# Adding the row term of a graph-attention layer with bf16 parts and a 0/1 map instead of small f32 matmuls

## The chip, the cores and the metric

The kernel runs on one NeuronCore of one Trainium2 chip. The metric is the device time of one execution in microseconds (us); the figure for a kernel is the median over its runs. The profile shows one such execution: the span from its first to its last instruction, and what each engine did in it. The engines are TensorE (PE, with its weight loads shown as PEld), VectorE (DVE), ScalarE (ACT), GpSimd (POOL) and SyncE (SP, which issues the DMAs here).

## The reference, cut to what matters

Sixteen graphs (`b`) of 1024 nodes with 64 features pass through two attention layers, each followed by a residual add and a layer norm. Each row of the adjacency matrix has a few non-zero entries. Layer 0 is an eight-head dot-product attention. Layer 1, which the change touches, is this:

```python
hp = einsum('bni,oi->bno', h, lin_w) + lin_b
W1, W2 = W_w[:, :64], W_w[:, 64:]
u = hp @ W1.T                       # one term for each row i
v = hp @ W2.T                       # one term for each column j
s = u[:, :, None, :] + v[:, None, :, :]
s = where(s > 0, s, 0.2 * s)
e = einsum('bijf,f->bij', s, a)
e = where(adj > 0, e, -9e15)
h_prime = softmax(e, axis=2) @ hp
out = elu(h_prime)                  # then x + out, layer norm
```

## The kernel before

**Rows, groups and slots.** The 1024 rows of a graph are cut into 8 tiles of 128 rows; a tile holds 64 rows from each half of the graph, so partitions 0 to 63 belong to one half (`n` = 0) and 64 to 127 to the other. Eight neighbouring rows form a group (`GR` = 8; `NQ` = 8 groups in each half of a tile). For each group the kernel builds on the device a list of the columns that any of its rows needs; with the group's own eight rows this gives `SLOTS` = 120 slots to a group. A mask (bf16, 0 where the row has the edge of that slot, `NEG` = -2^100 elsewhere) says which of the group's slots belong to which row. If a list overflows, a second, full routine runs instead; in the runs shown it is only tested for.

**The two layers.** `prepare` builds the lists and `finish` the masks. `gather` (L504) fetches the features of all slots by a matmul of the features with 0/1 columns `f`, which DVE makes in `indicate` (L480, bf16, 2176 elements each). So that bf16 matmuls keep f32 accuracy, the features are split by `thirds` into three bf16 parts, `x3`, on POOL: copy to bf16 (L453), subtract (L456), copy, subtract, copy, one operation at a time. The gathered features land in `xg` (64 features on the partitions of each half, 8 groups by 120 slots).

In layer 1, `sums` computes `u` once for a graph (f32, PSUM to SBUF by DVE, L733). For each tile `own_rows` makes two things: `ub` on POOL (L738, f32, 128x512: the tile's `u`, copied to each of the 8 groups and multiplied by `in_q`, which is 1 where the row belongs to that group and 0 elsewhere) and `rw` on ACT (L743, f32, 128x120: the mask turned to 1 where the row has the slot and 0 elsewhere). `project` then computes, for each group, v of its slots plus u of the row that owns the slot: 4 f32 matmuls of 480 columns (L750) start the sums in the two PSUM tiles `pz`, and 16 f32 matmuls of 120 columns (L756), one for each group, add `ub` of that group times `rw`. A single f32 matmul leaves two records in the trace, so the page counts 32 for each call at L756. All of them work on a quarter of the PE array (64 rows by 64 columns) in the order of `CORNERS`, so that four in a row lie in different quarters.

After `project` comes the leaky ReLU: ACT `r` (L761), then DVE `r` (L762), twice each. Then `weigh` (L776) contracts with `a`, adds the mask, and DVE takes the row maximum; `exps` (ACT), `turn_weights` (PE transpose L790, DVE copy `eT` L792), `attend` (L801) follow one or two steps later. `weigh` and `turn_weights` share one PSUM buffer (tag "e", one buffer), so that L776 has to wait until `eT` of the tile before has been copied.

**The order.** All five engines run queues written out by hand in one loop over steps `g`; `t` = `g` mod 8 is the position of a step. Layer 0 works on tile `g`, layer 1 on tile `u` = `g` - 12. A step issues, among others: `project(u-1)`, `place(g,1)`, `gather(u,0)`, `turn_weights`, `turn`, `place(g,2)`, `weigh(u-1)`, `gather(u,1)`, `place(g,3)`, `indicate`, `own`, `own_rows(u)`, `attend`, `place(g,4)`, and in the next step `place(g,0)`, `score`, `divide`. `place` is where the pieces of list building for the next graph are put in (in particular L325, L363 to L371, L345, L378, L380 on DVE and L328 on POOL), and where one operation of the list `lists.side` is taken: this is how the `thirds` operations are spread, one to a place:

```python
            while self.side:
                if next(self.side[0], 0) is None:
                    break
                self.side.pop(0)
```

Each engine takes its instructions strictly in the order in which they were issued. `sums` of a graph is called at the end of the step with `t` = 3, the first `own_rows` of that graph stands in the step with `t` = 4, and its first `project` in that with `t` = 5.

Of the kernel before, what the change touches and what calls it, by code (L numbers as in the profile page):

```python
# [9 lines left out]
F32 = mybir.dt.float32  # L10
I32 = mybir.dt.int32
AF = mybir.ActivationFunctionType
ALU = mybir.AluOpType
# [3 lines left out]
NEG = -(2.0**100)  # L17
# [12 lines left out]
BF16 = mybir.dt.bfloat16  # L30
# [3 lines left out]
def kernel(  # L34
# [4 lines left out]
    nc = tc.nc  # L39
    B, N, D = x.shape  # L40
    H = edge_bias.shape[1]
    HD = H * D
    P = 128
    NT = N // P
# [16 lines left out]
    ones = cst.tile([P, P], F32, name="ones")  # L61
# [3 lines left out]
    def sub(n):  # L65
        return slice(n * D, n * D + D)
# [41 lines left out]
    for h in range(H):  # L108
        c, r = h // 2, sub(h % 2)
# [73 lines left out]
    NQ = D // GR  # L183
# [33 lines left out]
    in_q = fst.tile([P, NQ], F32, name="in_q")  # L217
# [32 lines left out]
    SLOTS = 2 * CAP2 + GR  # L250
# [9 lines left out]
    dbl = fast.enter_context(tc.tile_pool(name="g_dbl", bufs=2))  # L260
# [21 lines left out]
    inputs, started, edges, masks, late = {}, {}, {}, {}, {}  # L282
# [160 lines left out]
        nc.vector.tensor_tensor(bad, bad, fl, ALU.max)  # L443
        masks[b] = mask

    def thirds(src, tag, nm):

        t3 = dbl.tile([P, 3, NT, D], BF16, tag=tag, bufs=3, name=f"{tag}_{nm}")
        less = per.tile([P, NT, D], F32, tag="less", name=f"less_{tag}_{nm}")

        def parts(rest):
            for k in range(3):
                nc.gpsimd.tensor_copy(t3[:, k, :, :], rest)  # L453
                yield
                if k < 2:
                    nc.gpsimd.tensor_tensor(less, rest, t3[:, k, :, :], ALU.subtract)  # L456
                    rest = less
                    yield

        return t3, parts(src)  # L460

    class Tiles:
# [63 lines left out]
        def begin(self, x_):  # L526

            b = self.b
            px = ps_g.tile([P, 512], F32, tag="g", name=f"px{self.layer}_{b}")
            columns_T(px, x_)  # L530
            self.xT = dbl.tile([P, 512], F32, tag=f"xT{self.layer}", bufs=2 - self.layer, name=f"xT{self.layer}_{b}")
            nc.scalar.copy(self.xT, px)
            self.t3, parts = thirds(x_, "x3", f"{self.layer}_{b}")
            self.f, self.xg, self.xn = {}, {}, {}
            lists.side.insert(0, parts)

    def banks(tag, name):

        return [ps_s.tile([P, 4, SLOTS], F32, tag=tag, name=f"{name}_{n}") for n in range(2)]
# [177 lines left out]
    class Layer1(Tiles):  # L717
# [9 lines left out]
        def sums(self):  # L727
            pu = ps_g.tile([P, NT, D], F32, tag="g", name=f"pu_{self.b}")
            for t in range(NT):
                for n in range(2):  # L730
                    nc.tensor.matmul(pu[sub(n), t, :], self.xT[:, ts(t, D)], w1h[:, n, :], start=True, stop=True)
            self.u = dbl.tile([P, NT, D], F32, tag="u", bufs=1, name=f"u_{self.b}")
            nc.vector.tensor_tensor(self.u, pu, rows_b[:, 0:1, :].to_broadcast([P, NT, D]), ALU.add)  # L733

        def own_rows(self, t):
            nm = f"{self.b}_{t}"
            ub = dbl.tile([P, NQ, D], F32, tag="ub", name=f"ub_{nm}")
            nc.gpsimd.tensor_tensor(  # L738
                ub, self.u[:, t, :].unsqueeze(1).to_broadcast([P, NQ, D]), in_q.unsqueeze(2).to_broadcast([P, NQ, D]),
                ALU.mult,  # L740
            )
            rw = dbl.tile([P, SLOTS], F32, tag="rw", name=f"rw_{nm}")
            nc.scalar.activation(rw, masks[self.b][:, t, :], AF.Identity, bias=ones[:, 0:1], scale=-1.0 / NEG)  # L743
            self.rows_[t] = ub, rw

        def project(self, t):
            xg, (ub, rw) = self.xg[t], self.rows_.pop(t)
            pz = banks("s", f"pz_{self.b}_{t}")
            for n, c_ in CORNERS:
                nc.tensor.matmul(  # L750
                    pz[n][sub(c_), :, :], w2d[sub(n), :],
                    xg[sub(n), :, :].rearrange("p (g c) k -> p c g k", c=2)[:, c_, :, :], start=True, stop=False,
                )
            for p in range(4):
                for n, c_ in CORNERS:
                    nc.tensor.matmul(  # L756
                        pz[n][sub(c_), p, :], ub[sub(n), 2 * p + c_, :], rw[sub(n), :], start=False, stop=(p == 3)
                    )
            self.r[t] = [dbl.tile([P, 4, SLOTS], F32, tag="r", bufs=3, name=f"r_{self.b}_{t}_{n}") for n in range(2)]
            for n, r in enumerate(self.r[t]):  # L760
                nc.scalar.activation(r, pz[n], AF.Relu)  # L761
                nc.vector.scalar_tensor_tensor(r, pz[n], SLOPE / (1.0 - SLOPE), r, ALU.mult, ALU.add)  # L762
# [117 lines left out]
    lists = Lists()  # L880
    with tc.manual_schedule(engines={getattr(mybir.EngineType, e) for e in order}):
# [12 lines left out]
        for g in range(NT * B + LAG + 7):  # L894
            u = g - LAG
            b, t = divmod(g, NT)
# [472 lines left out]
```

## Time and profile before

| | |
|---|---|
| median of 3 runs | 2506.59 us (2506.02 to 2509.31) |
| profiled execution | 2508.34 us, span 2506.5 us, mean granted PE clock 0.987 |
| PE busy | 2296.7 us (92% of the span) |
| PEld busy | 1951.9 us (78%) |
| DVE busy | 1930.4 us (77%) |
| ACT busy | 1450.3 us (58%) |
| POOL busy | 1010.8 us (40%) |
| L756 | 4096 PE records, mean 263 ns |
| L738 on POOL | 128 instructions, mean 1209 ns |

A record's duration includes its way through the array, and four of them overlap, so the 263 ns at L756 are not what each adds: the starts of records and of the group that follows tell that. "Idle before" is the time for which an engine stood still before an instruction, with the one that let it go. Until about 290 us only the lists of the first graph and layer 0 run; from about 2360 us on only layer 1 is left.

### The profile page before, as it was taken

How to read it: one execution, taken by the hardware profiler on the slowest of the kernel's cores; microseconds unless marked ns; L12 is line 12 of the kernel's file. 1: busy time of each engine (PE TensorE's matmuls, PEld its weight loads, DVE VectorE, ACT ScalarE, POOL GpSimd, SP SyncE). 2: the span in 40 equal slices, each digit the busy share in tenths (PEclk: the TensorE clock that was granted, in tenths of full speed). 3: DMA queues.
4: the chain of work that ended last, by engine and by line, in shares of the span. 5: the costliest groups of instructions: out<-in, count | busy, mean ns of one | idle time of the engine just before them, and what ended most of it. 6: DMA issues, size and time to landing. Idle time of an engine off the chain costs nothing.

```text
span 2506.5 us, 111153 instructions
## 1 busy us (share of the span) xinstructions
PE 2296.7 (92%) x48706; PEld 1951.9 (78%) x48706; DVE 1930.4 (77%) x5237; ACT 1450.3 (58%) x4401; POOL 1010.8 (40%) x1490
## 2 busy tenths in 40 slices
PE   5377999999999999999999999999999999999996
PEld 3266778888887888878888887878888887888864
DVE  6586868888887888888788878878787887866543
ACT  0054565666565665656566665656566665666743
POOL 1033433535344353534445353444534444443431
PEclk9988999999999999999999999999999999999998
DMA  3313242333224233323324232332423233231211
GB/s 102 109 43 117 81 143 77 104 116 109 91 81 138 77 117 103 121 77 100 120 77 140 81 119 77 113 107 78 142 86 113 83 111 103 66 96 61 69 38 29
DMA packets 192705, 239.03 MB, mean 95 GB/s; under 512 B 91732, under 2 KB 157332, under 8 KB 192212
## 3 DMA queue, kind: packets, MB, share of 16 engines
q1 hardware_dynamic: 192212, 231.85, 30.3%
q8 instruction: 384, 6.29, 1.0%
q14 instruction: 109, 0.89, 0.1%
HBM read 226.58 MB, written 5.21 MB: 92 GB/s over the span
## 4 chain that ended last, share of the span: by engine, by line
PE 66%; DVE 25%; DMA 3%; ACT 2%; issue 2%; POOL 1%; SPq 0%; POOLq 0%; ACTq 0%; DVEq 0%
PE pg L504 21%; PE s L616 5%; PE pt L523 5%; PE z L668 5%; DVE r L762 4%; PE pz L750 4%; PE pp L658 4%; PE pa L801 4%; PE pq L599 4%; PE pz L756 4%; PE po L684 3%; PE e L776 3%; DVE f L480 3%; DMA ad<-in_adj_dram 2%; PE pat L334 2%
## 5 line engine op out<-in xcount | busy, mean ns | idle before, releaser
L504 PE MATMUL pg<-f,x 128*64 128x272 bf16 (+2 forms) x13312 | 806.1, 273 | 40.4 <-DVE f L480 34.6
L504 PEld LDWEIGHTS <-x 128*64 128x64 bf16 x13312 | 662.8, 109 | 119.2 <-issue 73.8
L650 POOL TENSOR_TENSOR ls<-ls,den 128x480 f32<-128x480 f32 x256 | 298.5, 1166 | 579.8 <-DVE den L649 577.0
L510 ACT COPY xg<-pg 128x448 f32<-128x448 f32 x512 | 271.8, 531 | 392.4 <-PE pg L504 392.2
L480 DVE TENSOR_SCALAR f<-cb,jrow 128x2176 bf16<-128x2176 bf16 x512 | 409.0, 843 | 1.2 <-DMA cb<-col_d 1.0
L642 ACT ACTIVATE ls<-ls,mx 128x120 f32<-128x120 f32 x1024 | 391.2, 386 | 0.0
L524 ACT COPY xn<-pt 120x512 f32<-120x512 f32 x512 | 277.9, 598 | 22.7 <-PE pt L523 21.0
L523 PE MATMUL pt<-ident,xg 128*120 128x128 f32 x2048 | 269.6, 274 | 0.4
L761 ACT ACTIVATE r<-pz 128x480 f32<-128x480 f32 x256 | 132.2, 568 | 220.3 <-PE pz L756 220.3
L523 PEld LDWEIGHTS pt<-ident,xg 128*120 128x120 f32 x2048 | 229.4, 138 | 7.3 <-ACT xg L510 2.8
L489 POOL COPY xg<-xT 128x64 f32<-128x64 f32 x256 | 98.8, 396 | 307.1 <-PE pt L523 307.1
L762 DVE SCALAR_TENSOR_TENSOR r<-pz,r 128x480 f32<-128x480 f32 x256 | 155.9, 651 | 74.9 <-ACT r L761 74.6
L624 DVE TENSOR_TENSOR sc<-s,rowc 128x480 f32<-128x480 f32 x256 | 155.5, 649 | 71.2 <-PE s L616 69.3
L642 ACT ACTIVATION_READ_ACCUMULATOR ls<-ls,mx 128x1 f32 x1024 | 194.5, 190 | 0.0
L558 POOL TENSOR_TENSOR rs<-mv,eps 128x2 f32<-128x2 f32 x128 | 32.3, 253 | 379.0 <-DVE den L649 299.4
L632 DVE SCALAR_TENSOR_TENSOR ls<-sc 128x480 f32<-128x480 f32 x256 | 175.7, 686 | 0.0
L633 DVE TENSOR_REDUCE mx<-ls 128x4 f32<-128x480 f32 x256 | 167.2, 653 | 8.8
L756 PEld LDWEIGHTS pz<-rw,ub 64*64 64x64 f32 x4096 | 118.8, 133 | 63.2 <-issue 62.2
L600 DVE TENSOR_TENSOR qp<-pq,qb 128x512 f32<-128x512 f32 x128 | 88.2, 689 | 102.2 <-PE pq L599 101.0
L668 PE MATMUL z<-w,xn 120*64 120x64 f32 x4096 | 160.2, 229 | 4.8 <-ACT w L660 4.0
L658 PE MATMUL pp<-ident,ls 128*120 128x128 f32 x1024 | 143.0, 281 | 22.9 <-POOL ls L650 16.0
L668 PEld LDWEIGHTS z<-w,xn 120*64 120x64 f32 x4096 | 139.0, 141 | 28.6 <-ACT w L660 26.0
(212 smaller groups left out, 4092.7 us busy)
## 6 DMA issues: line engine op xcount, KB each, us to landing
cb<-col_d SPq DMA_DIRECT2D x271, 544.0 KB
ad<-in_adj_dram SPq DMA_DIRECT2D x256, 256.0 KB
xs<-in_x_dram SPq DMA_DIRECT2D x32, 128.0 KB
rows_s<-slot_d SPq DMA_DIRECT2D x256, 14.0 KB
out_dram<-o SPq DMA_DIRECT2D x32, 128.0 KB
col_d<-col SPq DMA_DIRECT2D x128, 4.2 KB
dg<-in_adj_dram SPq DMA_DIRECT2D x32, 2.0 KB
slot_d<-slot SPq DMA_DIRECT2D x16, 28.0 KB
```

Of the source, the lines that this page charges most:

```text
L480: nc.vector.tensor_scalar(fj.rearrange("p s n q k -> p (s n q k)"), cb.rearrange("p s n q k -> p (s n q k)"), jrow[:, j : j + 1], None, AL ...
L504: nc.tensor.matmul(pg[sub(n), :, FIRST * a_ + lo : FIRST * a_ + to], self.t3[:, k, 4 * hs + 2 * a_ + j, :], f[j][:, 2 * hs + a_, n, :, lo:to],
L510: nc.scalar.copy(dst, pg)
L523: nc.tensor.transpose(pt[:, q, :], xg[:, 4 * m + q, :], ident)
L524: nc.scalar.copy(self.xn[t][:, ts(m, 4), :], pt)
L632: nc.vector.scalar_tensor_tensor(ls, scs[n], SLOPE, scs[n], ALU.mult, ALU.max)
L642: nc.scalar.activation(ls[:, q, :], ls[:, q, :], AF.Exp, bias=neg[:, q : q + 1], accum_out=den[:, q : q + 1])
L650: nc.gpsimd.tensor_tensor(ls, ls, den.unsqueeze(2).to_broadcast([P, 4, SLOTS]), ALU.mult)
L658: nc.tensor.transpose(pt[:, p, :], ls[:, p, :], ident)
L668: nc.tensor.matmul(zz[sub(n), q, :], xn[:, q, sub(n)], w_[n][:, q // 2, sub(q % 2)], start=True, stop=True)
L756: nc.tensor.matmul(pz[n][sub(c_), p, :], ub[sub(n), 2 * p + c_, :], rw[sub(n), :], start=False, stop=(p == 3))
L762: nc.vector.scalar_tensor_tensor(r, pz[n], SLOPE / (1.0 - SLOPE), r, ALU.mult, ALU.add)
```

## The change

`u` is split once for a graph into three bf16 parts `u3` by `thirds` (two buffers), whose five POOL operations (three of L453, two of L456, 128x512 each) go to the front of `lists.side` after `sums` at the end of `t` = 3. `own_rows` makes `rw` in bf16 on ACT first, and from it, on POOL, a map `rq` (bf16, 128x960: `rw` repeated for the 8 groups and multiplied by `in_q`). `project` adds `u` with 3 rounds of 4 bf16 matmuls of 480 columns, in place of 16 f32 matmuls of 120 columns; each takes one part of the tile's `u` as weights and the map of four groups as the moving operand. `ub` goes. On POOL `rq` stands where `ub` stood; it now follows an ACT instruction of the same step, which `ub` did not.

```diff
-    def thirds(src, tag, nm):
+    def thirds(src, tag, nm, bufs=3):
-        t3 = dbl.tile([P, 3, NT, D], BF16, tag=tag, bufs=3, name=f"{tag}_{nm}")
+        t3 = dbl.tile([P, 3, NT, D], BF16, tag=tag, bufs=bufs, name=f"{tag}_{nm}")
...
             nc.vector.tensor_tensor(self.u, pu, rows_b[:, 0:1, :].to_broadcast([P, NT, D]), ALU.add)
+            self.u3, parts = thirds(self.u, "u3", f"{self.b}", 2)
+            lists.side.insert(0, parts)
 
         def own_rows(self, t):
             nm = f"{self.b}_{t}"
-            ub = dbl.tile([P, NQ, D], F32, tag="ub", name=f"ub_{nm}")
+            rw = dbl.tile([P, SLOTS], BF16, tag="rw", name=f"rw_{nm}")
+            nc.scalar.activation(rw, masks[self.b][:, t, :], AF.Identity, bias=ones[:, 0:1], scale=-1.0 / NEG)
+            self.rows_[t] = rq = dbl.tile([P, NQ, SLOTS], BF16, tag="rq", name=f"rq_{nm}")
             nc.gpsimd.tensor_tensor(
-                ub, self.u[:, t, :].unsqueeze(1).to_broadcast([P, NQ, D]), in_q.unsqueeze(2).to_broadcast([P, NQ, D]),
-                ALU.mult,
+                rq, rw.unsqueeze(1).to_broadcast([P, NQ, SLOTS]), in_q.unsqueeze(2).to_broadcast([P, NQ, SLOTS]), ALU.mult
             )
-            rw = dbl.tile([P, SLOTS], F32, tag="rw", name=f"rw_{nm}")
-            nc.scalar.activation(rw, masks[self.b][:, t, :], AF.Identity, bias=ones[:, 0:1], scale=-1.0 / NEG)
-            self.rows_[t] = ub, rw
 
         def project(self, t):
-            xg, (ub, rw) = self.xg[t], self.rows_.pop(t)
+            xg, rq = self.xg[t], self.rows_.pop(t)
...
-            for p in range(4):
+            for k in range(3):
                 for n, c_ in CORNERS:
                     nc.tensor.matmul(
-                        pz[n][sub(c_), p, :], ub[sub(n), 2 * p + c_, :], rw[sub(n), :], start=False, stop=(p == 3)
+                        pz[n][sub(c_), :, :], self.u3[sub(n), k, t, :],
+                        rq[sub(n), :, :].rearrange("p (g c) k -> p c g k", c=2)[:, c_, :, :], start=False, stop=(k == 2),
                     )
```

## The prediction

> **What bounds the kernel now.** I read the page first: which engine is full, and what its end is made of.
>
> ```profile
> PE 2296.7 (92%) x48706; PEld 1951.9 (78%) x48706; DVE 1930.4 (77%) x5237; ACT 1450.3 (58%) x4401; POOL 1010.8 (40%) x1490
> PE 66%; DVE 25%; DMA 3%; ACT 2%; issue 2%; POOL 1%; SPq 0%; POOLq 0%; ACTq 0%; DVEq 0%
> ```
>
> PE is nearly full, but a quarter of the chain of waits runs through DVE. Where, the list of waits says:
>
> ```profile
> PE e L776 <- DVE eT L792: 73.2, 90, 1.9
> DVE r L762 <- ACT r L761: 74.6, 105, 2.1
> ```
>
> PE's one repeated stop is L776, which waits for the copy `eT`. That copy stands on DVE behind L762, which comes out of `project`. If DVE waits at L762, an earlier `project` brings all of that forward; if DVE comes late, an earlier `project` only lengthens PE's stop. L762 waited in 105 of 128 calls. By position, from the timeline of the middle graphs: DVE has 0.24 us of wait at L762 for t = 0, 2, 4, 6, and 1.2 and 1.0 us for t = 5 and 7; at t = 3 it comes without a gap (it starts 0.085 us before its predecessor's end), and at t = 1 with no gap or 0.15 us. PE's stop at L776 is 1.3, 0.15 to 0.8, 1.3, 0.87, 0.39, 0, 0 and 0.81 us for t = 0 to 7.
>
> The timeline of PE, t = 3, shows what the edited lines take:
>
> ```profile
> 1268.52 1.03 PE L750 MATMUL pz<-xg,w2d 64*64 64x480 f32 x8
> 1269.37 1.00 PE L756 MATMUL pz<-rw,ub 64*64 64x120 f32 x32
> 1270.30 1.59 PE L504 MATMUL pg<-f,x 128*64 128x272 bf16 x26
> ```
>
> From start to start L756 takes 0.93 us. Last come POOL and DVE around L738, first in t = 2 (with ACT), then DVE and POOL in t = 0:
>
> ```profile
> 1260.77 1.05 POOL L738 TENSOR_TENSOR ub<-u,in_q 128x512 f32<-128x512 f32 x1
> 1261.77 0.60 POOL L453 CAST x<-y 128x512 bf16<-128x512 f32 x1
> ```
> ```profile
> 1260.95 0.92 DVE L366 TENSOR_TENSOR left<-left,left 128x32 int32<-128x32 int32 x1
> 1261.90 0.52 DVE L368 SCALAR_TENSOR_TENSOR kb<-left,c 128x32 f32<-128x32 int32 x1
> 1262.34 1.47 DVE L480 TENSOR_SCALAR f<-cb,jrow 128x2176 bf16<-128x2176 bf16 x2
> 1263.74 0.17 DVE L363 TENSOR_SCALAR left<-left 128x32 int32<-128x32 int32 x1
> 1263.94 0.19 DVE L364 TENSOR_TENSOR left<-left,left 128x32 int32<-128x32 int32 x1
> 1264.38 0.19 DVE L366 TENSOR_TENSOR left<-left,left 128x32 int32<-128x32 int32 x1
> ```
> ```profile
> 1261.18 0.44 ACT L743 ACTIVATE rw<-mask,ones 128x120 f32<-128x120 bf16 x1
> ```
> ```profile
> 1226.04 2.74 DVE L325 TENSOR_SCALAR ab<-ad 128x512 bf16<-128x512 int32 x4
> ```
> ```profile
> 1225.49 1.54 POOL L738 TENSOR_TENSOR ub<-u,in_q 128x512 f32<-128x512 f32 x1
> 1227.39 1.11 POOL L328 TENSOR_TENSOR ab<-ab,no_diag 128x128 bf16<-128x128 bf16 x2 [0.36 <-DVE ab L325]
> ```
>
> The same L366 takes 0.92 us beside L738 and 0.19 alone: it ends 0.05 us after L738 does; L368 behind it ends 0.05 us after L453. In t = 0, L738 itself takes 1.54 instead of 1.04 us, since it starts under an L480, and the first of the four L325 takes 1.27 instead of 0.42 us. So DVE's two-operand, conversion and indicator operations and POOL's exclude each other; MAX8, MATCH_REPLACE8 and the readers of PSUM keep their usual times.
>
> **What PE gains.** In the records four quarters start together, and the next four after 102.5 ns (L756, 120 columns in f32) or 403 ns (L750, 480 columns, second round); the bf16 mask matmuls of L616, in the same quarters with 120 columns, follow every 52.5 ns, so f32 costs twice bf16 for each record, with 2.5 ns on top. Old: 8 rounds of 102.5 = 820 ns, and 110 ns until L504 can follow (0.93 in all). New: 3 rounds of 480 bf16 columns at 200 + 2.5 = 608 ns, the 110 unchanged, as after L616. From f32 to bf16 L616 loses nothing (103 ns from the last f32 round to the first bf16 one). Saving 0.21 us; by L504's mean (1.52 us for 3264 columns, 0.465 ns each) a round is 223 ns and the saving 0.15. I take 0.21, as L616 has the same shape; at most it is worth 128 x 0.21 = 27 us.
>
> It counts where DVE waits at L762. At t = 0, 2, 4, 6 the room is 0.24 + 0.085 = 0.32 us, above 0.21; at 5 and 7 there is plenty. It does not count at t = 1 and 3 while lists are being built, 13 graphs each, so 26 steps; in the last 12 steps something else applies. Of the 116 steps ahead of them 90 count: 90 x 0.21 = **19 us**.
>
> **What POOL's longer instruction costs.** POOL's f32 products take 0.40 us for 128 elements (L563) and 1.04 for 512 (L738): 1.67 ns an element. 960 make 1.78 us; with the slope from L328 in bf16 (0.42 for 128) to L456 (1.16 for 512, mixed types) it is 2.0. I take 1.9, 0.86 more than `ub`. Its wait for `rw` costs little: the ACT instruction ends before or some 0.8 us after POOL's old start, behind L524 and ahead of L673. Queued behind it on POOL are L453, L328 and the next step's L650; POOL idled for 1.6 to 5.6 us before L650 at all positions but t = 6, where L650 slips 0.8 us and the second one's 1.0 us of idle takes it up. `project` needs the map 2 us or more after its end. Without this cover each would cost up to 0.9 us.
>
> DVE pays in two places:
> - t = 2, into t = 3. `rq` can start only after `rw` (1261.62). L366 and L368 then run free, and DVE reaches its first L480 at 1261.29, to 1262.07. `rq` gets in behind it and holds until about 1263.8; the second L480 follows to 1264.5, L453 to 1265.0, and L364 ends near 1265.1 instead of 1264.13. If the second L480 goes first, the loss is 0.55. From 0.55 to 1.1; I take 0.85. DVE has no wait until L762 of t = 3, and PE stops there already, so it counts in full: 13 x 0.85 = **11 us**.
> - t = 0, into t = 1. The third L325 ends 0.86 us later and L624 some 0.75; 0.24 is free at L762, leaving 0.51. But in six of 13 graphs an adjacency load (DMA) came later than that anyway (t = 1 lasts 19.26 us at the shortest and up to 21.3). The mean over the graphs is 0.28: **3.6 us**, between 0 and 0.51 each (7).
>
> At the other positions the longer map meets cover: DVE idle for 4.1 us (t = 1), MAX8 and MATCH_REPLACE8 (t = 3, 4), 0.46 and 1.47 us idle (t = 5), 1.0 us at the next L762 (t = 6), 3.3 us idle (t = 7).
>
> **The split of u** adds 3 x 0.61 + 2 x 1.16 = 4.2 us on POOL for a graph. The first copy goes ahead of L650 in t = 4 (3.2 us of idle), three operations into POOL's 3.8 us before the second L489 of t = 4, the last behind `rq`. They hold up L480 by some 1.3 us, under DVE's 1.9 us of idle before L624. Nothing, or 16 x 0.5 = 8 us if that cover fails.
>
> **The tail.** In the last 12 steps (mostly 9.25 us each) nothing hides the map:
>
> ```profile
> 2448.71 1.04 POOL L738 TENSOR_TENSOR ub<-u,in_q 128x512 f32<-128x512 f32 x1
> 2448.91 0.40 ACT L743 ACTIVATE rw<-mask,ones 128x120 f32<-128x120 bf16 x1
> 2451.01 1.00 PE L756 MATMUL pz<-rw,ub 64*64 64x120 f32 x32
> ```
>
> `rq` starts at 2449.39 (after `rw` and 0.08) and ends at 2451.2 to 2451.4; with 0.07 to reach PE the matmuls start 0.25 to 0.45 late and take 0.21 less. 12 x 0.14 = **1.7 us** lost.
>
> **Sum.** 19 - 11 - 3.6 - 1.7 = 3 us gained: 2508.3 becomes 2505.3 for the profiled execution, which lies 1.75 above the median of the runs; for the median 2506.6 - 3 = 2503.6. A change of 0.2% (5 us) is about what a measurement of this kernel can tell from none, so the likeliest is "the same", barely.
>
> A rule of the Trainium skill speaks against the change: "GPSIMD Engine Reference", section "Elementwise — side-by-side cycle accounting", has a two-operand f32 operation of 2048 elements at 4497 ns, 2.2 ns an element, where the rows here give 1.67. By it the map would take 2.1 us and the sum would end near 2510.
>
> **Rivals.**
> - *DVE is not held up* (faster). If DVE's operations win the order or the map is short, half the 14.6 us stay: 2497; with none lost 2489. For it: L366 and L368 are freed, DVE runs ahead by 1.05 us. Against: L738 got in ahead of a waiting L325 each time. 0.34.
> - *The map holds DVE and the tail for longer* (slower). Each 0.1 us more costs 1.3 us at t = 3, 0.7 at t = 1 and 1.2 in the tail, 3.2 in all. It decides from 2.0 us (break-even), and beyond 2.15 us it is slower by over 0.2%; at 2.3 us it gives 2516. For it: no row here writes bf16 from a repeated bf16 operand, and L456 with mixed types is dearer than L738. Against: L328 in bf16 costs what f32 does. 0.26.
> - *Four streams of 480 bf16 columns do not run together.* In pairs the rounds take 1.2 us and each step loses 0.4: about +50 us. L616 and L504 speak against it. 0.02.
>
> The rest, 0.38, is the forecast, between 2501.6 and 2511.6. That the change does not do what it says is excluded: it puts 12 bf16 matmuls in place of the 16.
>
> **How the numbers follow.** Chances: faster 0.34, same 0.38, slower 0.28. The range takes in half of the losses gone with some of the steps t = 1 gaining too (2491) and a map of 2.25 us (2515).
>
> **What would show it.** Right: the new u matmuls take 0.72 us from start to start; POOL's map 1.8 to 2.0 us; L776's stop at t = 3 grows from 0.87 to about 1.9 us while t = 0, 2, 4 keep theirs; t = 5 and 6 last 0.21 us less; L364 or L366 at t = 2 last over 1 us. Wrong: stops unchanged at t = 3, L762 without a wait at even t, a map over 2.15 us, or PE waiting for POOL ahead of L776.

## The result and the profile after

The change makes no measurable difference: the ratio of after to before is 1.0004 [0.9993, 1.0015], with medians of 2507.47 us for after (2500.86 to 2516.06, 12 runs) and 2506.65 us for before (2502.98 to 2510.03, 12 runs beside them). The profiled execution of after took 2500.86 us (span 2499.1), which is its fastest run and 6.6 us under its median. So the two profiles are compared step by step here, and the total is taken from the medians.

The page of after, the lines for engines and for the chain of waits by engine:

```profile
PE 2274.5 (91%) x46146; PEld 1887.6 (76%) x46146; DVE 1956.6 (78%) x5237; ACT 1450.0 (58%) x4401; POOL 1192.9 (48%) x1570
PE 61%; DVE 32%; issue 2%; DMA 2%; POOL 1%; ACT 1%; SPq 0%; POOLq 0%; ACTq 0%; DVEq 0%
```

PE has lost 22 us of work and POOL has gained 182. DVE has 26 us more busy time with the same 5237 instructions, so some of its instructions have become longer. In the chain, PE has given up 5% of the span and DVE has taken 7%.

The list of waits (us in total, times, longest):

```profile
PE e L778 <- DVE eT L794: 85.2, 90, 1.9
DVE r L764 <- ACT r L763: 48.7, 45, 2.3
```

DVE now waits for `project` in 45 calls instead of 105, and PE's stop at `weigh` has grown by 12 us. DVE waits less for PE, and PE waits more for DVE. (Lines have moved: L750 is now L751, L756 L757, L762 L764, L776 L778 and `eT` L792 is L794.)

PE at t = 2 (start, duration, engine and line, operation, operands, count, idle before in brackets):

```profile
1246.17 1.04 PE L751 MATMUL pz<-xg,w2d 64*64 64x480 f32 x8
1247.03 0.79 PE L757 MATMUL pz<-rq,u 64*64 64x480 bf16 x12
1247.75 1.58 PE L504 MATMUL pg<-f,x 128*64 128x272 bf16 x26
...
1251.99 0.62 PE L778 MATMUL e<-r,a_two 128*32 128x120 f32 x16 [1.52 <-DVE eT L794]
```

From start to start L757 takes 0.72 us (1247.03 to 1247.75), as forecast. The stop at L778 is 1.52 us, where before had 1.31 at this position: PE arrives 0.21 us earlier and waits 0.21 us longer.

DVE and POOL later in the same step, beside the new map:

```profile
1256.56 0.19 DVE L366 TENSOR_TENSOR left<-left,left 128x32 int32<-128x32 int32 x1
1256.79 0.19 DVE L368 SCALAR_TENSOR_TENSOR kb<-left,c 128x32 f32<-128x32 int32 x1
1256.89 3.01 DVE L480 TENSOR_SCALAR f<-cb,jrow 128x2176 bf16<-128x2176 bf16 x2
1259.82 0.58 DVE L363 TENSOR_SCALAR left<-left 128x32 int32<-128x32 int32 x1
1260.44 0.19 DVE L364 TENSOR_TENSOR left<-left,left 128x32 int32<-128x32 int32 x1
```
```profile
1257.32 2.00 POOL L743 TENSOR_TENSOR rq<-rw,in_q 128x960 bf16<-128x960 bf16 x1 [0.91 <-ACT rw L741]
1259.27 1.10 POOL L453 CAST x<-y 128x512 bf16<-128x512 f32 x1
```

L366 and L368 run free now (0.19 us each; L366 had 0.92). The map starts under the first L480, and the second L480 waits for its end: the pair takes 3.01 us instead of 1.47. L363 behind it is held by L453 (0.58 instead of 0.17).

In t = 0 the map stands beside L325. Four of these take 3.48 us where they took 2.74 in before:

```profile
1221.19 3.48 DVE L325 TENSOR_SCALAR ab<-ad 128x512 bf16<-128x512 int32 x4
```

The table gives the length of each step from `project` to the next `project`, by position, as the median over the 12 graphs in the middle, and the sum over the last 12 steps; first before, then what each kernel of this study differs from it (us). The readings by position below come from it; the kernels are described with the experiments. What DVE and POOL do late in one step shows in the length of the next.

| kernel | t=0 | 1 | 2 | 3 | 4 | 5 | 6 | 7 | last 12 |
|---|---|---|---|---|---|---|---|---|---|
| before | 17.38 | 19.47 | 17.95 | 19.12 | 17.00 | 16.95 | 15.56 | 20.74 | 118.13 |
| after | 0 | +.26 | -.01 | +.88 | -.23 | -.21 | -.21 | -.23 | -.50 |
| short map | 0 | -.15 | -.01 | +.07 | -.23 | -.21 | -.21 | -.23 | -2.38 |
| long `ub` (before) | +.01 | +.26 | -.01 | +.75 | 0 | +.09 | +.01 | 0 | +.36 |
| swap | -.62 | +.26 | -.62 | +.87 | -.23 | -.21 | -.21 | -.23 | -.52 |
| swap (before) | -.39 | +.23 | -.40 | +.01 | 0 | 0 | 0 | 0 | +.03 |
| swap, late map | -.62 | +1.17 | -.62 | -.21 | -.23 | -.21 | -.08 | +1.24 | -.51 |
| late map alone | 0 | +1.17 | -.01 | -.21 | -.22 | -.21 | -.17 | +1.22 | -.52 |
| swap, late f32 map | -.41 | +1.17 | -.41 | -.22 | -.01 | -.01 | -.02 | +1.22 | +1.78 |
| swap, late map, six loads | -.62 | -.36 | -.62 | -.21 | -.23 | -.21 | -.21 | +1.22 | -.52 |
| the same, t = 6 at its old place | -.61 | -.36 | -.62 | -.21 | -.22 | -.21 | -.21 | +.66 | -.52 |
| the same with an f32 map | -.41 | -.22 | -.41 | -.21 | -.01 | -.01 | -.02 | +.87 | +1.80 |
| swap, six loads (before) | -.40 | -.21 | -.40 | 0 | +.01 | 0 | -.01 | 0 | +1.50 |
| swap, six loads | -.62 | +.26 | -.62 | +.87 | -.23 | -.21 | -.21 | -.23 | -.49 |

In after, four positions gain PE's 0.21 to 0.23 us, two gain nothing and two lose: the means over a graph's eight steps differ from before's by 0.0 us in sum.

**The theory after the result.** PE's 0.21 us is real. It is paid back at t = 3 and 1 because the map holds DVE, and it does not arrive at t = 0 and 2 because something on DVE, not `project`, sets when `eT` comes. For the second part the two timelines of t = 2 give a candidate. DVE, then POOL, of after:

```profile
1248.45 1.22 DVE L764 SCALAR_TENSOR_TENSOR r<-pz,r 128x480 f32<-128x480 f32 x2
...
1250.45 0.79 DVE L353 TENSOR_SCALAR flags<-lst 128x4 f32<-128x4 f32 x1
...
1251.65 0.28 DVE L794 COPY eT<-pt 120x128 f32<-120x128 f32 x1
```
```profile
1250.22 0.99 POOL L650 TENSOR_TENSOR ls<-ls,den 128x480 f32<-128x480 f32 x1
```

and DVE, then POOL, of before (its clock of the span is 4.39 us later at this step):

```profile
1255.07 0.56 DVE L353 TENSOR_SCALAR flags<-lst 128x4 f32<-128x4 f32 x1
...
1256.04 0.28 DVE L792 COPY eT<-pt 120x128 f32<-120x128 f32 x1
```
```profile
1254.61 0.99 POOL L650 TENSOR_TENSOR ls<-ls,den 128x480 f32<-128x480 f32 x1
```

L353 handles 4 elements a partition and lasts 0.79 us: it ends at 1251.24, just after POOL's product L650 (1251.21). In before it started 0.23 us later in the step, lasted 0.23 us less, and `eT` was copied at the same moment of the step. So L650, which ends at the same moment of the step in both, seems to set it; it is the product of `divide(g-2, 1)`, queued on POOL behind the norm of layer 0 (L558 to L563). The rivals: the map alone is to blame for all of it, or a PE saving of 0.21 us is worth little anywhere.

### The profile page after: what moved, and what is told of

The parts are those of the page before. It is cut to its first block, busy times and chain, and to the rows that moved or that the text cites. A ratio compares the mean times of both kernels' runs of the same rounds, so it can differ in the third digit from the quotient of the medians.

```text
span 2499.1 us, 106105 instructions
## 1 busy us (share of the span) xinstructions
PE 2274.5 (91%) x46146; PEld 1887.6 (76%) x46146; DVE 1956.6 (78%) x5237; ACT 1450.0 (58%) x4401; POOL 1192.9 (48%) x1570
## 4 chain that ended last, share of the span: by engine, by line
PE 61%; DVE 32%; issue 2%; DMA 2%; POOL 1%; ACT 1%; SPq 0%; POOLq 0%; ACTq 0%; DVEq 0%
PE pg L504 20%; PE pt L523 5%; PE s L616 5%; DVE r L764 4%; PE z L668 4%; DVE f L480 4%; PE pp L658 4%; PE pa L803 4%; PE pq L599 4%; PE po L684 3%; PE e L778 3%; DVE ab L325 2%; PE pz L751 2%; PE pat L334 2%; DVE qp L600 2%
## 5 line engine op out<-in xcount | busy, mean ns | idle before, releaser
L504 PE MATMUL pg<-f,x 128*64 128x272 bf16 (+2 forms) x13312 | 806.2, 273 | 35.5 <-DVE f L480 34.5
L504 PEld LDWEIGHTS <-x 128*64 128x64 bf16 x13312 | 662.9, 110 | 144.1 <-issue 96.2
L650 POOL TENSOR_TENSOR ls<-ls,den 128x480 f32<-128x480 f32 x256 | 292.9, 1144 | 424.4 <-DVE den L649 423.2
L480 DVE TENSOR_SCALAR f<-cb,jrow 128x2176 bf16<-128x2176 bf16 x512 | 441.1, 905 | 0.4 <-DMA cb<-col_d 0.2
L743 POOL TENSOR_TENSOR rq<-rw,in_q 128x960 bf16<-128x960 bf16 x128 | 240.4, 1878 | 59.6 <-ACT rw L741 59.6
L489 POOL COPY xg<-xT 128x64 f32<-128x64 f32 x256 | 114.0, 459 | 228.7 <-PE pt L523 228.7
L558 POOL TENSOR_TENSOR rs<-mv,eps 128x2 f32<-128x2 f32 x128 | 32.3, 252 | 374.4 <-DVE den L649 299.0
L764 DVE SCALAR_TENSOR_TENSOR r<-pz,r 128x480 f32<-128x480 f32 x256 | 155.7, 649 | 49.5 <-ACT r L763 48.7
L632 DVE SCALAR_TENSOR_TENSOR ls<-sc 128x480 f32<-128x480 f32 x256 | 179.3, 700 | 0.0
```

What stands on the lines that cost most here:

```text
L480: nc.vector.tensor_scalar(fj.rearrange("p s n q k -> p (s n q k)"), cb.rearrange("p s n q k -> p (s n q k)"), jrow[:, j : j + 1], None, AL ...
L504: nc.tensor.matmul(pg[sub(n), :, FIRST * a_ + lo : FIRST * a_ + to], self.t3[:, k, 4 * hs + 2 * a_ + j, :], f[j][:, 2 * hs + a_, n, :, lo:to],
L632: nc.vector.scalar_tensor_tensor(ls, scs[n], SLOPE, scs[n], ALU.mult, ALU.max)
L650: nc.gpsimd.tensor_tensor(ls, ls, den.unsqueeze(2).to_broadcast([P, 4, SLOTS]), ALU.mult)
L743: nc.gpsimd.tensor_tensor(rq, rw.unsqueeze(1).to_broadcast([P, NQ, SLOTS]), in_q.unsqueeze(2).to_broadcast([P, NQ, SLOTS]), ALU.mult)
```

## The experiments

**A map of half the length, and a `ub` of nearly twice the length.** The first edits after: the map, in two tiles `maps` that are zero from the start, covers four of the eight groups, so that `u` is left out for the other four. The second edits before: `ub` writes 960 elements on POOL, of which `project` uses 512.

```diff
-            self.rows_[t] = rq = dbl.tile([P, NQ, SLOTS], BF16, tag="rq", name=f"rq_{nm}")
+            self.rows_[t] = rq = maps[t % 2]
             nc.gpsimd.tensor_tensor(
-                rq, rw.unsqueeze(1).to_broadcast([P, NQ, SLOTS]), in_q.unsqueeze(2).to_broadcast([P, NQ, SLOTS]), ALU.mult
+                rq[:, 0:4, :], rw.unsqueeze(1).to_broadcast([P, 4, SLOTS]),
+                in_q[:, 0:4].unsqueeze(2).to_broadcast([P, 4, SLOTS]), ALU.mult
             )
```
```diff
-            ub = dbl.tile([P, NQ, D], F32, tag="ub", name=f"ub_{nm}")
+            ub = dbl.tile([P, 15, D], F32, tag="ub", name=f"ub_{nm}")
             nc.gpsimd.tensor_tensor(
-                ub, self.u[:, t, :].unsqueeze(1).to_broadcast([P, NQ, D]), in_q.unsqueeze(2).to_broadcast([P, NQ, D]),
+                ub, self.u[:, t, :].unsqueeze(1).to_broadcast([P, 15, D]), in_15.unsqueeze(2).to_broadcast([P, 15, D]),
```

> The changed kernel, with POOL's map operation cut from 960 to 480 elements a step (four of the eight groups written, the other four left at zero from the start; this leaves out u for half of the groups). PE, ACT and DVE instructions as in the changed kernel. Theory (PE's 0.21 us a step are real and are paid back on DVE, which POOL's longer map keeps out of the memory it shares with it): the map takes about 1.0 us, L364 at t = 2 ends where it did before, the stops of L778 at t = 1 and 3 no longer grow, the gain at t = 4 to 7 (about 60 steps x 0.21 = 13 us) and in the tail (2 us) is kept: about 2492 us, 0.994 of before. Rival (the gain is lost in PE's own queue or elsewhere, the map's length does not matter): no change against the changed kernel, about 2507.

> The kernel before, with POOL's ub widened from 512 to 960 elements a step (seven more groups of 64 that no one reads), all else as before. Theory: it takes 1.78 us, L366 and L368 at t = 2 are held 0.75 us longer and L325 at t = 0 as well; t = 3 lasts 0.75 us longer in 13 graphs (10 us), t = 1 about 0.3 (4 us), no gain on PE: about 2520 us, 1.005. Rival (POOL idles 60% of the time, so its length is hidden): same, 2507.

Measured beside before's median of 2507.84 us (11 runs, as for the next pair): 2490.55 us, 0.9933 [0.9919, 0.9947], for the short map, and 2523.77, 1.0057 [1.0043, 1.0071], for the long `ub`. In the table the short map, against after, takes 0.81 us off t = 3, 0.41 off t = 1 and 1.9 off the last 12 steps, and changes no other position: with 13 graphs this makes 17.7 us, and the medians are 17 apart. The long `ub` adds 0.75 and 0.26 at the same two positions (and 0.09 at t = 5), with PE's work as it was. So the length of POOL's instruction is what costs at t = 1 and 3, in both directions. (At t = 1 the median also moves with the adjacency loads: the swap below moves it by 0.23 us in before, where POOL's instruction is the old one. The last experiment has t = 1 without these waits.) It is not the whole story: with the short map t = 0 and 2 still gain nothing.

**The product ahead of the norm.** `divide(g-2, 1)`, with its L650, is issued ahead of layer 0's residual and norm, in after and in before:

```diff
-            at(l0, g - 3, "residual")
             at(l0, g - 2, "divide", 1)
+            at(l0, g - 3, "residual")
```

> The changed kernel, with divide(g-2, 1) issued ahead of layer 0's residual instead of behind it: on DVE its reciprocal comes ahead of the norm's statistics, on POOL its product L650 ahead of the norm's four operations. Theory (at t = 0 and 2 PE's gain was lost because DVE's L353 or L431, ahead of the copy eT, stands until POOL's L650 has ended, and L650 does not come from project): L353 and L431 take 0.2 us instead of 0.79, the stops of L778 at t = 0 and 2 fall from 1.51 to about 0.9 us: 26 x 0.6 = 16 us, about 2491. Rival (L353 and L431 are long by themselves, or the stop is set by what follows them): no change, 2507.

> The kernel before with the same exchange of divide and residual. Theory: L353 and L431 take 0.2 us instead of 0.55, the stops of L776 at t = 0 and 2 fall by 0.35 to 0.4 us: 26 x 0.38 = 10 us, about 2497, which is less than the same edit brings in the changed kernel, since there project's gain is set free as well. Rival: no change, 2507.

Measured: 2488.09 us, 0.9909 [0.9895, 0.9924], in after, and 2491.01, 0.9926 [0.9909, 0.9944], in before. DVE and POOL at t = 2 of the changed kernel with the swap:

```profile
1242.54 0.16 DVE L353 TENSOR_SCALAR flags<-lst 128x4 f32<-128x4 f32 x1
...
1243.12 0.28 DVE L794 COPY eT<-pt 120x128 f32<-120x128 f32 x1
```
```profile
1239.63 0.99 POOL L650 TENSOR_TENSOR ls<-ls,den 128x480 f32<-128x480 f32 x1 [3.77 <-DVE den L649]
```

L650 ends before L353 starts, L353 takes 0.16 us, and `eT` comes 0.58 us after it instead of 1.20. At t = 0 and 2 the steps become 0.62 us shorter in the changed kernel and 0.39 in before; the difference, some 0.22, is PE's saving, which now arrives at these positions too. This settles the second part of the theory. That before gains 16.8 us by the same edit was more than expected. In its profile the 12 middle graphs are 9.6 us shorter, as expected, but they also start 7.8 us earlier, and what shortened the start is not shown. Most of the swap's worth does not need the change.

**The map one step later.** The map is needed only by the `project` of the following step. Here `own_rows` of layer 1 moves to that step, behind the first four exponentials of layer 0, with the swap and without; the last 12 steps keep the old place.

```diff
             at(l0, g - 2, "exps", 0, range(4))
+            if g < NT * B:
+                at(l1, u - 1, "own_rows")
...
-            at(l1, u, "own_rows")
+            if g + 1 >= NT * B:
+                at(l1, u, "own_rows")
```

> The changed kernel with the exchange of divide and residual, and with own_rows of a tile issued one step later, behind the first four exponentials of layer 0 (in the last 12 steps where it was): rw then comes late on ACT and POOL's map falls beside DVE's MAX8, L624 and L633, which it does not hold up. Theory: at t = 2 L364 to L368 and L480, at t = 0 L325 run free of the map; the stops of L778 at t = 3 and t = 1 fall below those of the kernel before, t = 3 lasts 1.7 us less than in the changed kernel and t = 1 some 0.5: 13 x 2.2 = 29 us below the run with the exchange alone, about 2460. Rival (t = 3 is long because of the split's or the cast's operations, or because of L480 itself): 2488 as with the exchange alone.

> The changed kernel with own_rows one step later, without the exchange. Theory: t = 3 and t = 1 as in the run with both, t = 0 and 2 as in the changed kernel (L353 and L431 stand until L650 ends): 29 us below the changed kernel, about 2478. Rival: the two places are one queue, and what is saved at t = 3 and 1 comes back: 2507.

Measured beside 2507.64 us (16 runs, as for the next two experiments): 2490.23 us, 0.9931 [0.9918, 0.9945], with the swap (30 us over what was expected) and 2515.37, 1.0027 [1.0015, 1.0039], without (37 over). At t = 3 the expectation held: from +0.87 to -0.21 us, all of the loss and PE's saving too. But t = 7 lost 1.24 us and t = 1 lost 1.17 instead of gaining. At t = 7 the map stands behind layer 0's norm on POOL and now meets L632 (POOL, then DVE, of the version with six loads below, which has the same loss there):

```profile
1300.61 1.78 POOL L743 TENSOR_TENSOR rq<-rw,in_q 128x960 bf16<-128x960 bf16 x1
```
```profile
1300.99 1.92 DVE L632 SCALAR_TENSOR_TENSOR ls<-sc 128x480 f32<-128x480 f32 x1
```

L632 takes 1.92 us where the one before it took 0.83. At t = 1 DVE's L325, which the map no longer holds, comes to the adjacency loads before they have landed: its waits for `ad` rise from 23.0 us in 22 cases (swap alone) to 42.1 in 40. In both some 20 us of that lie in the first 270 us, so in the repeated steps the waits rise from 2.7 us to 21.5.

**PE's saving undone, the map kept.** The version with swap and late map again, with an f32 map, no split of `u` (which has two buffers here), and one round of four f32 matmuls of 480 columns, whose two passes cost PE what the old 16 did:

```diff
-            for k in range(3):
-                for n, c_ in CORNERS:
-                    nc.tensor.matmul(
-                        pz[n][sub(c_), :, :], self.u3[sub(n), k, t, :],
+            for n, c_ in CORNERS:
+                nc.tensor.matmul(
+                    pz[n][sub(c_), :, :], self.u[sub(n), t, :],
```

> As the run before, but map and u in f32: no split, and four f32 matmuls of 480 columns add u (2 records each, 2 rounds of 403 ns) in place of twelve in bf16 (3 rounds of 203 ns). POOL, ACT and DVE as there but for the split's five operations a graph. Theory: the u matmuls take 0.92 us from start to start instead of 0.72; where DVE does not hold PE each step pays 0.2 us: 15 to 25 us above the run before, about 2480. Rival (with DVE out of the way something else sets the steps and PE's 0.2 us is not seen): the same as the run before, or less by the split's POOL time.

Measured: 2512.39 us, 1.0021 [1.001, 1.0031], which is 22 us above the same order with bf16 parts. The u matmuls take 0.92 us from start to start instead of 0.72. The table puts it at t = 0, 2, 4 and 5 (0.20 to 0.22 each) and in the last 12 steps (2.3 us). By the medians t = 1, 3 and 7 change by 0.02 us at most, but t = 1, where the loads come late, lasts 0.41 us longer by the mean. So the rival that PE's saving is worth little anywhere falls: with the swap and the map moved, four of the eight positions show all of it, and the last 12 steps most of it.

**Six adjacency buffers.** To take the loads out of t = 1, two more are sent ahead:

```diff
-                ads[k] = dbl.tile([P, 2, SEG], I32, tag="ad", bufs=4, name=f"ad_{b}_{hs}_{T}")
+                ads[k] = dbl.tile([P, 2, SEG], I32, tag="ad", bufs=6, name=f"ad_{b}_{hs}_{T}")
...
-        for k in range(4):
+        for k in range(6):
...
-                load(hs * NT + T + 4)
+                load(hs * NT + T + 6)
```

> The run with both edits, with six instead of four buffers for the adjacency blocks, loaded two blocks further ahead. Theory: L325 at t = 0 and 1 no longer stands for a load (up to 2 us in some graphs); t = 1 becomes the same in all graphs: 0 to 10 us less than with both edits, and a smaller spread between runs. Rival (the loads land late because the DMA queue is full of them, not because they start late): no change.

Measured: 2459.75 us, 0.9814 [0.9801, 0.9827], 30 us less than with four buffers, where at most 10 were expected. L325's waits for loads fall from 42.1 us to 3.6 (list of waits, swap with late map, then this version):

```profile
DVE ab L325 <- DMA ad<-in_adj_dram: 42.1, 40, 2.3
```
```profile
DVE ab L325 <- DMA ad<-in_adj_dram: 3.6, 5, 1.2
```

By the step's starts half of the 30 us lies in the graphs (t = 1: 1.53 us less by the median, 1.07 by the mean) and half ahead of them: the first step of the middle graphs starts at 320.6 instead of 336.1 us, since the lists of the first graph wait for the same loads: before 270 us L325's waits fall from 20.7 us to 3.6, and behind that none is left. The expectation had left out that start.

**The collision at t = 7.** Of t = 6 the map goes back to its old place (`t != 7` in the first condition of the late map, `or t == 6` in the second), with bf16 parts and with the f32 map.

> The run with exchange, late own_rows and six adjacency buffers, but own_rows of the step t = 6 back at its old place: there, late, the map stood behind the norm's operations on POOL and held L632 for 1.3 us, which made t = 7 1.45 us longer than in the changed kernel. Theory: t = 7 falls back to 20.5 us, 13 x 1.45 = 19 us: about 2441. Rival (t = 7 is long for another reason, the statistics on DVE or L428): no change, 2460.

> As the run before, with map and u in f32 (no split, four f32 matmuls of 480 columns in place of twelve in bf16). Theory: PE's 0.2 us a step is paid where DVE does not hold PE: 15 to 25 us above the run before, about 2461. Rival: the same as the run before.

Measured beside 2507.94 us (9 runs, as for the last pair): 2454.62 us, 0.9796 [0.9774, 0.9817], the lowest median of this study, and 2477.73, 0.9889 [0.9869, 0.9908]. The f32 map costs 23 us again. Of the 19 us expected from the move only 5 came, and the intervals with and without it overlap. At t = 7 the step is 0.56 us shorter, where 1.45 were expected, and stays 0.66 above before. The timeline of DVE, then POOL, in that step points to the reason, for t = 7's own map, which is also late:

```profile
1313.32 1.70 DVE L428 TENSOR_SCALAR mask<-rows_s,code 128x896 bf16<-128x896 bf16 x1
```
```profile
1312.98 1.79 POOL L743 TENSOR_TENSOR rq<-rw,in_q 128x960 bf16<-128x960 bf16 x1 [2.19 <-ACT rw L741]
```

L428, which makes the masks of the next graph, takes 1.70 us in 13 of its 16 calls and 0.44 in all 16 when the map is at its old place. Laid beside the version with the old place, everything in that step runs level until L428; from there DVE is 1.05 us late, and PE is 0.90 late from `gather` on. The map back at its old place for t = 7 as well would be the next thing to try; it was not run, so L428's part is read from the timeline and not tested.

**The change with and without, in the better order.** Swap and six buffers, in before and in after, `own_rows` at its old place:

> The kernel before with the exchange of divide and residual and six adjacency buffers. Theory: against the exchange alone (2491) the graphs whose L325 stood for a load lose that wait, 0.5 us in the mean at t = 1: about 2484. Rival (the six buffers were what brought the run with both edits down, not the order of the map): about 2460.

> The changed kernel with the exchange and six adjacency buffers, own_rows at its old place. Theory: t = 3 keeps its 20.0 us, only the waits for loads go: about 2482. Rival (six buffers alone bring 28 us): about 2460.

Measured: 2472.74 us, 0.9869 [0.985, 0.9889], and 2469.72, 0.9856 [0.9833, 0.9878]. Against the swap alone six buffers bring 18 us in each by the medians, 14 and 13 by the ratios (each to before's runs beside it), where 7 and 6 were expected. Most of it lies ahead of the first middle graph, whose start moves by 16.5 and 17.6 us in the profiles; the expectations had left out the start again. The change itself is worth 3 us here, less than the two intervals can tell apart; its steps at t = 3 and 1 pay as in after. In the repeated steps L325 no longer waits for a load in either kernel, so t = 1 shows what the map costs there: 0.47 us (from -0.21 to +0.26). With the map moved, except at t = 6, the change and the move together are worth 18 us (2472.74 to 2454.62). `ub` was not moved in before, so how much of this before would gain from such a move alone is open; in the order with the map moved it is the f32 map, 23 us slower, that shows what the bf16 matmuls are worth.

## Why the prediction was right, and where a step failed

"The same" held, at 2507.47 us against a forecast of 2503.6, inside the range. It was right partly by luck: two errors, 5.5 us too much gain and 2.2 us too much loss, went against each other, and the range was wide beside a change of a few us.

- **What PE gains.** 0.72 us from start to start, as worked out: three bf16 rounds of 203 ns (at t = 3, where `project` is held up, 1.01). t = 4 to 7 last 0.21 to 0.23 us less.
- **The step that failed: the count of 90.** The prediction let PE's 0.21 us count at t = 0 and 2 because DVE waited 0.24 us at L762. It did arrive at L764 there (that wait is now 0.01 us), but not at `eT`. The working looked at DVE's wait before `r` only, and not at what DVE does between `r` and `eT`: L353 at t = 2 (and L431 at t = 0), held by POOL's L650, which `project` does not release. Its list of what would show it right had the stops of t = 0 and 2 unchanged; they grew from 1.30 to 1.51 us. 26 steps of 0.21 us did not come: 5.5 us. L353's 0.56 us in before, against 0.16 of L354, the same operation right behind it, was there to be read.
- **What POOL's map costs.** The map takes 1.79 us by the median (1.9 taken; the line through the two f32 products had given 1.78). The Trainium skill ("GPSIMD Engine Reference", "Elementwise — side-by-side cycle accounting") has 4497 ns for a two-operand f32 operation of 2048 elements, from which 2.1 us is an estimate for 960; the measurement, 1.79, decides. At t = 3 the step got 0.88 us longer (0.85 taken), by the second L480 waiting for the map, as the working had it. The sign that went with it, L364 or L366 over 1 us at t = 2, did not show: both stay at 0.19. And only 0.17 of it is at L778 (0.86 to 1.03 us), where 1.0 was forecast. In one middle graph, laid beside before, PE takes 0.29 us more from L757 to L504 than the 0.72 and loses 0.66 ahead of L792 first, where the list of waits of after now has a line with 8.9 us (before: 1.2 in 3 cases):

```profile
PE pt L792 <- DVE den L649: 8.9, 16, 0.6
```

At t = 1 the step lost 0.26 by the median and 0.14 by the mean (0.28 taken); without waits for loads it was 0.47, where the working had 0.51.
- **The tail.** It was to lose 1.7 us and gained 0.5. The mechanism held: from the sixth of the 12 steps on L757 starts when the map has ended (POOL, then PE):

```profile
2450.64 1.79 POOL L743 TENSOR_TENSOR rq<-rw,in_q 128x960 bf16<-128x960 bf16 x1 [0.69 <-ACT rw L741]
2452.49 0.80 PE L757 MATMUL pz<-rq,u 64*64 64x480 bf16 x12
```

That is mostly 1.06 instead of 0.86 us behind the start of L751, so 0.20 late where 0.25 to 0.45 was forecast, and PE's 0.21 makes it up: five of these seven steps keep their length within 0.03 us, two lose 0.11 and 0.17. Of the five ahead of them, where the map is in time, four gain 0.21 and one nothing. With the short map eleven of the 12 gain 0.20 to 0.23.
- **The split of u** shows no loss at t = 4.

With these terms put right, 64 steps of 0.21 us (13.4) and 0.5 in the tail stand against 13 x 0.88 (11.4) and 13 x 0.14 to 0.26 (1.8 to 3.4). The balance lies between 0.9 us lost and 0.7 gained, beside a measured 0.8 lost (the interval allows 1.8 gained to 3.8 lost). What stays open is why the profiled execution of after is 6.6 us under its own median: no other execution of it was profiled. Its span is 7.4 us below before's, and none of that lies in the 12 middle graphs: they start 3.9 us earlier, and the 16 steps between them and the last 12 are 3.6 us shorter. Adjacency loads, which vary by a microsecond from step to step at t = 1, are a possible source, not a shown one.

The prediction's reading that some of DVE's operations and POOL's exclude each other was the core of it and held in the runs shown here. The Trainium skill states this as a rule ("SBUF — State Buffer", "Who interferes with whom"): DVE and GpSimd share a pair of ports, which DVE needs in its two-port modes and for a second input from SBUF; whoever issues first has it for the whole instruction, and the other stands. The rows agree, down to the 0.16 us L353 that took 0.79 beside L650. Readers of PSUM were not held: the 128 `eT` copies of after take 0.26 to 0.29 us, also the 71 that start while a POOL product runs.

## What to carry to other kernels

A saving on the busiest engine counts only as far as the wait it shortens is the last one: follow the chain from the edited line through everything that stands on the other engine up to the next hand-over, and look there for instructions that are longer than their size (4 elements in 0.56 us). Where two engines exclude each other, price an added instruction by what stands on the other engine beside it, and expect a moved one to meet something else: the map, moved out of t = 2, held L632 and then L428. An order that frees the held engine is worth more than the saving, and decides whether the saving is seen: the change was worth 3 us, within the noise, with the map at its old place, and 18 together with the move of most of it.

## What the runs showed of the hardware that was not expected

- A DVE operation of 4 elements on 128 partitions (0.16 us) stands for up to 0.6 us while a POOL product runs and ends when the product does (L353 beside L650).
- POOL's product of two bf16 operands, 960 elements, takes 1.78 us at the least and 1.79 at the median, and so does the f32 map of the same size. The type makes no difference that can be seen.
- Two more buffers for one input load were worth 13 to 18 us in a kernel whose page puts DMA at 3% of the chain of waits; most of it lies in the start, before the repeated steps.
